# Order of the work around the paired 3x3 convolutions of a pre-activation block, and both rows' products in one tile

## The chip, the cores and the metric

The kernel runs on one core of a Trainium2 chip. The metric is the device time of one execution in microseconds, here the median of three runs. The engines are TensorE (PE in the profile, with its weight loads as PEld), VectorE (DVE), ScalarE (ACT), GpSimd (POOL) and SyncE (SP, which issues DMA transfers).

## The reference

A batch of 8 images with 512 channels of 32 x 32 pixels goes through group norm, a 1x1 convolution (cv1), two bottleneck layers, each with a 3x3 convolution, an attention over the 1024 pixels and a 1x1 convolution (m_cv2), and a closing 1x1 convolution (cv2). All of it is fp32.

```python
def _gn(v, G=32, eps=1e-5): ...        # group norm: (v - mean) / sqrt(var + eps)
def cbs(x, w, p, pad):                 # conv, batch norm with fixed statistics, SiLU
    return silu(bn_eval(conv2d(x, w, pad), p))
def bot_attention(x, qkv_w, rw, rh):   # HEADS = 4, HD = 64, hw = 1024
    q, k, v = conv2d(x, qkv_w, 0) ...
    logits = einsum('bhdi,bhdj->bhij', q, k + (rw + rh)) * HD ** -0.5
    return einsum('bhij,bhdj->bhdi', softmax(logits), v)
t = cbs(_gn(x), cv1_w, cv1_bn, 0)      # 512 -> 512 channels, 1x1
ys = [t[:, :256], t[:, 256:]]
for i in range(2):                     # two layers
    z = cbs(ys[-1], m_cv1_w[i], m_cv1_bn[i], 1)      # 3x3, 256 -> 256
    z = bot_attention(z, m_qkv_w[i], m_rw[i], m_rh[i])
    z = silu(bn_eval(conv2d(z, m_cv2_w[i], 0), m_cv2_bn[i]))
    ys.append(ys[-1] + z)
out = x + cbs(concatenate(ys, axis=1), cv2_w, cv2_bn, 0)   # 1024 -> 512
```

## The kernel before, in words

**Stages.** The images are taken in four pairs (loop `for p in range(NP)`), image a and image b. A pair passes, for layer 0 and then layer 1, these stages: `conv3x3` (line 486) for both images at once; `project_strassen` (684) and `attention_fast` (778) of image a; the same of image b; and `m2` (1021), the 1x1 convolution with its SiLU and the addition to the layer's input, for each image. Between the stages of layer 0 lies cv1 of the next pair's images (`strassen_cv1`, 1140; plain `cv1` in the first pair), and at the end of layer 1 cv2 of both images (`strassen`, 1053, in seven block products), in the last image plain. What the last pair does is the same without a next pair. Layer 1's order is: convolution, project a, attention a, project b, m2 a, attention b, m2 b, with cv2 around it.

**The 3x3 convolution** is of the Winograd kind: input tiles of 6 x 6 pixels are transformed by `tiles_in` (421) on VectorE, the filters by `make_u` (342), and the products of transformed input and filter are summed on TensorE and transformed back on VectorE. `tiles_in` works for one image and one or several of three row indices i; each gives three tiles `v_in` (cp = 0, 1, 2 for the column indices (0, 5), (1, 2), (3, 4)). In `conv3x3` a unit is an output block oc and a row index i, six in a convolution; a unit has two rows. Before, each row takes a tile `ps` of two PSUM banks for its own six products (L520); ACT copies products 2 and 4 (L524), and VectorE takes sum and difference with 1 and 3 (L526, L527) and joins products 0 and 5 (L528). These operate on 128 x 256 elements. Four recombinations (`c_r`, L533 to L536) and the keeping of both rows (`c_k`, L539 and further; output to `z`, L542 to L551) follow. The pool `ps_big` has three tiles of two banks, which all stages share; `ps_av` has one.

**Attention.** `attention_fast` computes 16 pairs of steps per image: logits (L801), exp on ACT (L805), addition of the exponentials on VectorE (L819, L821), products with v (L835). The softmax's denominators are made on TensorE (`sums`, 845), written to DRAM by way of `s_row`, read back as a narrow tile, inverted (`reciprocal` on 128 x 8), written and broadcast back to 128 x 512 (`spread`, 891), and used by `scale` (904, L907). There are four groups; the last one is done without DRAM, by `last_sums` (862), an addition, and a 128 x 512 reciprocal (L943). `behind` is a dictionary of hooks, called at fixed steps of the attention: group g, or (g, quarter).

**What sets the order.** The program text is in the order of the wishes, and a scheduler gives each engine its queue; `tc.issue_after(ins)` puts what is inside behind an instruction. A tile pool with few buffers makes a later tile wait for the release of an earlier one. Filters, weights and new filter blocks share a ring of ten slots (tag `u`); `feed` issues loads of keys on SP, `take` uses them. The first pair also makes the layer-1 filters (`make_u`, with `load_raw`, stored by POOL) and the block sums of the weights. The group norm of the next image (`group_norm`, 614) is stepped by the hooks; its last step, `apply`, normalises on VectorE (L624).

**What the text below touches**: the names above; `first_sum` (678), which forms the first block sum of the projection's input (`t_z`, L681, L732 to L734), and `L697`/`L701`, the products of the projection; `next_cv1` with `begin`, `go_on`, `rest`, the steps of the next image's cv1.

## Time and profile before

| what | value |
|---|---|
| median of three runs | 2467.01 us (2465.4 to 2467.69) |
| the profiled execution's own time | 2468.43 us |
| its span | 2467.0 us |
| mean granted TensorE clock | 0.973 |
| ACT 128 x 1024 exponentials (L805) | 512 of 1023 ns |
| VectorE additions of exponentials (L821) | 384 of 1223 ns |

The span is the time from the first to the last instruction of the profiled execution. A row of the table of costliest groups gives line, engine, operation, output from inputs, sizes and count; after the first bar the busy time in us and the mean duration in ns; after the second the time that the engine sat idle just before these instructions, and what ended most of it. The table by windows gives the busy time of each engine in a stretch, so that a stage can be read by itself. In the text, "layer 0" and "layer 1" are the bottleneck layers, and "a" and "b" the two images of a pair.

### The profile page before, as it was taken

To read this page: it belongs to the slowest core of one execution; us is meant where nothing else is said; L and a number is where in the kernel's file an instruction comes from. 1 tells how busy PE (TensorE), PEld (TensorE's weight loads), DVE (VectorE), ACT (ScalarE), POOL (GpSimd) and SP (SyncE) were. 2 spreads that over 40 slices of the span, in tenths; PEclk is the share of its full clock that TensorE was granted. 3 is DMA by queue.
4 is the path that set the end of the run, shared out by engine and by line. 5 is a ranking of instruction groups with operands and counts; after the bars stand their busy time and mean duration, and the time that the engine had idled before them with its cause. 6 is when DMAs were issued, how large, how long until landed. Compare 5 with 4: busy or idle time off the path is not lost.

```text
span 2467.0 us, 40820 instructions
## 1 busy us (share of the span) xinstructions
PE 2261.3 (92%) x16378; PEld 1107.8 (45%) x16378; DVE 1991.3 (81%) x2942; ACT 1013.0 (41%) x1345; POOL 177.1 (7%) x405
## 2 busy tenths in 40 slices
PE   6697979899998999999999998989999898989998
PEld 2362424634447343644346443463444733363433
DVE  6988786888868989887788889888786879597763
ACT  4134333265313545255511555436531364425541
POOL 4101110000010010000011000000001000000002
PEclk9898989999999999999999999999999999999999
DMA  8533423521245041522145223341124502141103
GB/s 309 184 119 126 158 93 110 183 66 65 67 159 192 28 170 41 178 78 78 32 145 185 82 74 113 117 156 57 40 78 155 182 23 78 49 157 36 53 27 121
DMA packets 126534, 268.93 MB, mean 109 GB/s; under 512 B 33440, under 2 KB 62560, under 8 KB 125312
## 3 DMA queue, kind: packets, MB, share of 16 engines
q1 hardware_dynamic: 102256, 181.41, 22.8%
q0 software_dynamic: 24080, 84.82, 9.4%
q8 instruction: 131, 2.15, 0.3%
q14 instruction: 67, 0.55, 0.1%
HBM read 197.10 MB, written 69.07 MB: 108 GB/s over the span
## 4 chain that ended last, share of the span: by engine, by line
PE 56%; DVE 21%; issue 16%; ACT 3%; DMA 2%; POOL 1%; SPq 0%; DVEq 0%; POOLq 0%; ACTq 0%
PE av_ps L835 14%; PE l_ps L801 13%; PE c L1047 8%; PE c_new L1047 4%; PE p_ps L697 4%; PE m_ps L1027 4%; PE ps L416 3%; PE pv_ps L701 1%; PE c_ps L520 1%; DVE acc L821 1%; PE x_ps L1153 1%; DVE w_d L466 1%; DVE v_in L469 1%; PE s_ps L852 1%; DVE c_t L526 1%
## 5 line engine op out<-in xcount | busy, mean ns | idle before, releaser
L805 ACT ACTIVATE pt<-l_ps 128x1024 f32<-128x1024 f32 x512 | 495.7, 1023 | 352.8 <-PE l_ps L801 317.1
L821 DVE TENSOR_TENSOR acc<-acc,pt 128x1024 f32<-128x1024 f32 x384 | 469.6, 1223 | 79.5 <-ACT pt L805 54.6
L801 PE MATMUL l_ps<-q,kr 64*64 64x512 f32 x4096 | 494.5, 597 | 28.6 <-ACT pt L805 25.8
L835 PE MATMUL av_ps<-pt,vT 64*64 64x512 f32 x4096 | 492.5, 597 | 16.0 <-DVE z L843 11.3
L801 PEld LDWEIGHTS l_ps<-q,kr 64*64 64x64 f32 x4096 | 158.4, 134 | 305.4 <-issue 247.1
L520 PE MATMUL c_ps<-v_in,u 128*64 128x128 f32 x4320 | 254.4, 282 | 38.8 <-DVE c_e L528 38.2
L835 PEld LDWEIGHTS av_ps<-pt,vT 64*64 64x64 f32 x4096 | 158.6, 134 | 291.5 <-issue 234.8
L520 PEld LDWEIGHTS c_ps<-v_in,u 128*64 128x64 f32 x4320 | 249.1, 143 | 47.6 <-ACT c_m L524 41.9
L697 PE MATMUL p_ps<-t_z,sq 128*128 128x512 f32 x256 | 130.1, 628 | 27.5 <-DVE c_e L528 19.6
L524 ACT COPY c_m<-c_ps 128x256 f32<-128x256 f32 x96 | 35.2, 370 | 254.1 <-PE c_ps L520 137.1
L1027 PE MATMUL m_ps<-z,m_sb 128*128 128x512 f32 x256 | 113.6, 595 | 0.2
L819 DVE TENSOR_TENSOR acc<-pt 128x1024 f32<-128x1024 f32 x64 | 78.1, 1221 | 38.2 <-ACT pt L805 38.2
L697 PE MATMUL p_ps<-z,sq 128*128 128x512 f32 x192 | 92.2, 604 | 15.3 <-ACT z L397 14.0
L397 ACT ACTIVATE t<-m_ps,bh,sh 128x512 f32<-128x512 f32 x64 | 46.3, 775 | 108.8 <-PE m_ps L1027 108.5
L1027 PEld LDWEIGHTS m_ps<-z,m_sb 128*128 128x128 f32 x256 | 47.8, 190 | 61.7 <-issue 55.0
L697 PEld LDWEIGHTS p_ps<-t_z,sq 128*128 128x128 f32 x256 | 45.8, 200 | 62.7 <-issue 56.1
L701 PEld LDWEIGHTS pv_ps<-sq,z 128*128 128x128 f32 x384 | 51.3, 197 | 33.8 <-issue 18.4
L701 PE MATMUL pv_ps<-sq,z 128*128 128x128 f32 x384 | 53.4, 284 | 10.4 <-DVE z L843 7.7
L907 DVE TENSOR_TENSOR z<-z,rs 128x512 f32<-128x512 f32 x64 | 43.9, 687 | 22.3 <-DMA rs<-r_dram 22.0
L466 DVE TENSOR_TENSOR w_d<-w_rows 128x1024 f32<-128x1024 f32 x48 | 58.6, 1222 | 3.7 <-POOL w_rows L452 1.3
L416 PE MATMUL ps<-x,w 128*128 128x512 f32 x128 | 56.1, 594 | 0.0
L1153 PE MATMUL x_ps<-t_x,sw 128*128 128x512 f32 x128 | 55.6, 592 | 0.0
(276 smaller groups left out, 3228.3 us busy)
## 6 DMA issues: line engine op xcount, KB each, us to landing
u<-u SPq DMA_DIRECT2D x135, 512.0 KB
sq<-sq SPq DMA_DIRECT2D x48, 384.0 KB
x_res<-in_x_dram POOLq DMA_DIRECT2D x63, 256.0 KB, 4.1
x<-in_x_dram SPq DMA_DIRECT2D x28, 512.0 KB
y_in<-y SPq DMA_DIRECT2D x28, 512.0 KB
u<-u_new POOLq DMA_DIRECT2D x54, 256.0 KB, 2.8
rs<-r_dram SPq DMA_DIRECT2D x96, 128.0 KB
v<-v_new POOLq DMA_DIRECT2D x36, 256.0 KB, 3.3
```

The costliest lines, as they stand in the source:

```text
L416: last_product[0] = nc.tensor.matmul(ps[:, half, :], w_of(k), rhs_of(k, half), start=(k == begin), stop=(k == end))
L466: tt(d, e[:, :, 2 : F + 2], e[:, :, 0:F], ALU.subtract)
L520: nc.tensor.matmul(to[o], us[cp][:, k, row, c, o], rhs, start=(k == 0), stop=(k == NM - 1))
L697: nc.tensor.matmul(ps[:, o, :], w[:, o, :], rhs, start=not onto, stop=True, skip_group_check=onto)
L701: nc.tensor.matmul(v[:, ts(j, P)], rhs[:, ts(j, P)], w[:, 2, :], start=j == 0 and not onto, stop=True, skip_group_check=True,)
L801: nc.tensor.matmul(ps[kh * HD : (kh + 1) * HD, hd, :], kr[r, c, o : o + HD], q[r, c, ts(half, HALF)], start=True, stop=True,)
L805: exp = nc.scalar.activation(pt, ps, AF.Exp, scale=SCALE)
L821: ins = nc.vector.tensor_tensor(accs[g], accs[g], pt[i], ALU.add)
L835: nc.tensor.matmul(avs[g][hd * HD : (hd + 1) * HD, kh, :], vT[r, j, o : o + HD], pt[i][r, hd, :], start=(j == 0), stop=(j == NJ - 1),)
L1027: nc.tensor.matmul(pss[oc][:, half, :], m2_sb[:, n, k, ts(oc, P)], ao[:, k, ts(half, HALF)], start=(k == 0), stop=(k == NM - 1),)
L1047: nc.tensor.matmul(ps[:, o, :], w[:, k, ts(o, P)], rhs[part][:, c], start=(k == 0 and not onto), stop=(k == KB - 1), skip_group_check=onto,)
L1153: nc.tensor.matmul(ps[:, o, :], w[:, c, ts(o, P)], rhs[c], start=(c == 0 and not onto), stop=(c == 1), skip_group_check=onto,)
```

## The change

- **Convolution.** The two rows of a unit are now in one tile each for the products 1 to 4 (`inner_ps`, both banks) and for 0 and 5 (`outer_ps`, one bank). TensorE makes products 1 to 4 of both rows first. The ACT copy and the three VectorE operations become 128 x 512 each, half as many. The order in which filters are fed is cp = 1, 2, 0.
- **Input side.** `tiles_in` goes by row index over both images: at the start of the kernel index by index, and at the end of a pair indices 0 and 1 of both images ahead of cv2's last part (`b3`), index 2 behind it.
- **Normalisation.** In the first pair, `group_norm` normalises by eight ACT activations per image, and no longer by four VectorE operations.
- **Filters.** `make_u` yields two or three times per chunk instead of once. One key of the layer-1 filters is made in the first pair's attention a, three between attention a and in attention b; before, two in each.
- **Ends of attention.** Unless `at_once` is set, the last group too goes through `sums`, `spread` and `scale`, each called by the caller. Only attention b of layer 0 keeps the direct form.
- **m2 of image a.** In layer 1, and in layer 0 of the last pair, `sums` is called within the first product of project b (`early`), and `spread`, `scale`, `m2` and the loading of the Exp table after its first half (`middle`). In layer 0 of the other pairs these steps stand between parts of the next image's cv1. At the end of layer 1 cv2's first part is cut in two around them.
- `rs` has four buffers instead of two, and the sums for cv1's Strassen products (`t_x`) are formed after its first products.

The core of the diff:

```diff
-    SLOTS = ((0, 1), (2, 4), (3, 5))
...
-        return [("u", n, oc, i, cp) for oc in range(NM) for i in range(NI) for cp in range(3)]
+        return [("u", n, oc, i, cp) for oc in range(NM) for i in range(NI) for cp in (1, 2, 0)]
...
+            if i < 2:
+                yield last
             nc.scalar.activation(u0, c0, AF.Identity, scale=0.25)
             nc.scalar.copy(u5, c2)
             tt(u2, c0, c2, ALU.add)
             tt(u1, u2, c1, ALU.add)
-            tt(u2, u2, c1, ALU.subtract)
+            yield tt(u2, u2, c1, ALU.subtract)
...
-                    e = act.tile([P, 2, 2, q], F32, tag="rs", name="c3_e", bufs=2)
-                    for row in range(2):
-                        ps = ps_big.tile([P, 2, HALF], F32, tag="big", name="c3_ps")
-
-                        def slot(a, b):
-                            bank, at = divmod(a, 4)
-                            return ps[:, bank, at * q : (at + b - a) * q]
-
-                        for cp in range(3):
-                            for c in range(2):
-                                to = slot(SLOTS[cp][c], SLOTS[cp][c] + 1)
-                                for k in range(NM):
-                                    rhs = vs[i, cp][:, c].rearrange(
-                                        "p g (r t k s) -> p g r t k s", r=2, t=NT, k=NM
-                                    )[:, :, row, :, k]
-                                    for h in range(2):
-                                        o = slice(h * HD, (h + 1) * HD)
-                                        nc.tensor.matmul(
-                                            to[o], us[cp][:, k, row, c, o], rhs, start=(k == 0), stop=(k == NM - 1)
-                                        )
-                        m24 = act.tile([P, 2, q], F32, tag="h", name="c3_m", bufs=2)
-                        nc.scalar.copy(m24, slot(4, 6).rearrange("p (a q) -> p a q", a=2))
-                        m13 = slot(2, 4).rearrange("p (a q) -> p a q", a=2)
-                        tt(m[:, row, 0::2], m13, m24, ALU.add)
-                        tt(m[:, row, 1::2], m13, m24, ALU.subtract)
-                        stt(
-                            e[:, row].rearrange("p a q -> p (a q)"), slot(0, 2), -6.0,
-                            m[:, row, 0:2].rearrange("p a q -> p (a q)"), ALU.mult, ALU.add,
-                        )
+                    e = act.tile([P, 2, 2, q], F32, tag="rs", name="c3_e", bufs=4)
+                    inner_ps, outer_ps = (
+                        ps_big.tile([P, 2, HALF], F32, tag="big", name="c3_ps") for _ in range(2)
+                    )
+
+                    def slots(ps, bank):
+                        return ps[:, bank, : 4 * q].rearrange("p (r a q) -> p r a q", r=2, a=2)
+
+                    places = {
+                        1: (inner_ps, 0, 0), 2: (inner_ps, 1, 0), 3: (inner_ps, 0, 1), 4: (inner_ps, 1, 1),
+                        0: (outer_ps, 0, 0), 5: (outer_ps, 0, 1),
+                    }
+                    for cps in ((1, 2), (0,)):
+                        for row in range(2):
+                            for cp in cps:
+                                for c in range(2):
+                                    ps, bank, at = places[CPS[cp][c]]
+                                    to = slots(ps, bank)[:, row, at]
+                                    for k in range(NM):
+                                        rhs = vs[i, cp][:, c].rearrange(
+                                            "p g (r t k s) -> p g r t k s", r=2, t=NT, k=NM
+                                        )[:, :, row, :, k]
+                                        for h in range(2):
+                                            o = slice(h * HD, (h + 1) * HD)
+                                            nc.tensor.matmul(
+                                                to[o], us[cp][:, k, row, c, o], rhs,
+                                                start=(k == 0), stop=(k == NM - 1),
+                                            )
+                    m24 = act.tile([P, 2, 2, q], F32, tag="h", name="c3_m", bufs=2)
+                    nc.scalar.copy(m24, slots(inner_ps, 1))
+                    tt(m[:, :, 0::2], slots(inner_ps, 0), m24, ALU.add)
+                    tt(m[:, :, 1::2], slots(inner_ps, 0), m24, ALU.subtract)
+                    stt(
+                        e.rearrange("p r a q -> p r (a q)"),
+                        slots(outer_ps, 0).rearrange("p r a q -> p r (a q)"), -6.0,
+                        m[:, :, 0:2].rearrange("p r a q -> p r (a q)"), ALU.mult, ALU.add,
+                    )
...
-        def group_norm(xts):
+        def group_norm(xts, on_act=False):
...
-            yield apply(range(NX), gm, gn_rstd(dev)[0])
+            gr, _, _ = gn_rstd(dev)
+            if not on_act:
+                yield apply(range(NX), gm, gr)
+                return
+            shift = small.tile([P, NX], F32, tag="dev", name="shift")
+            nc.gpsimd.tensor_tensor(shift, gm, gr, ALU.mult)
+            nc.gpsimd.tensor_scalar(shift, shift, -1.0, None, ALU.mult)
+            for c in range(NX):
+                for half in range(NH):
+                    part = xts[c][:, ts(half, HALF)]
+                    nc.scalar.activation(part, part, AF.Identity, scale=gr[:, c : c + 1], bias=shift[:, c : c + 1])
+            yield
...
-        def project_strassen(n, z, w, t):
+        def project_strassen(n, z, w, t, early=None, middle=None):
...
+            product(ps_a, ps_v[:, 0], w["11"], b11, between=early)
...
+            if middle:
+                middle()
...
+            if not at_once:
+                with tc.issue_after(added.ins):
+                    scale(g - 1, rss.pop(g - 1))
+                return SimpleNamespace(
+                    sums=lambda: s_drams.update({g: sums(g)}),
+                    spread=lambda: rss.update({g: spread(g, s_drams[g])}),
+                    scale=lambda: scale(g, rss.pop(g)),
+                )
...
-        for g in range(G):
-            s.tiles_in(Y1[g], putter(vs, g), [0])
-        for g in range(G):
-            s.tiles_in(Y1[g], putter(vs, g), [1, 2])
+        ecs = [{}, {}]
+        for i in range(NI):
+            for g in range(G):
+                s.tiles_in(Y1[g], putter(vs, g), [i], ecs[g])
...
+        def hooks(norms, every=1):
+            calls = {}
+            for g in range(NG):
+                for at in range(4):
+                    key = (g, at) if at else g
+                    calls[key] = [step_norm] if key in norms else []
+                    if (4 * g + at) % every == 0:
+                        calls[key].append(step_u)
+            return {key: (lambda fs: lambda: [f() for f in fs])(fs) for key, fs in calls.items()}
+
+        NORMS = (1, 2, (2, 2), 3)
+        if p == 0:
+            more_u = filters([(0, 0, 0)])
...
-        scaled, check = s.attention_fast(qkv, z[:, :, 0], at_of(ia, 0), behind)
-        if p == 0:
-            for made in chunks:
-                pass
-        last = s.m2(0, z[:, :, 0], Y1[0], lambda oc, half: inner(Y2[0], oc, half))
-        if more:
-            nxt.rest()
-        with tc.issue_after(last.ins):
-            check()
+            before = behind[3, 2]
+            behind[3, 2] = lambda: (before(), make_sq(1, q_tiles, [t[:, j] for t in q_sums for j in range(2)]))
+        end = s.attention_fast(qkv, z[:, :, 0], at_of(ia, 0), behind)
+        for made in more_u:
+            pass
...
+            more_u = filters([(0, 1, 1), (1, 0, 1), (1, 1, 1)])
+
+        def m2_a():
+            return s.m2(0, z[:, :, 0], Y1[0], lambda oc, half: inner(Y2[0], oc, half))
+
+        if more:
+            end.sums()
+            nxt.go_on()
+            nxt.sums()
+            end.spread()
+            nxt.rest(0)
+            end.scale()
+            last = m2_a()
+            for i in range(1, 4):
+                nxt.rest(i)
...
+            for _ in range(12):
+                step_u()
...
+            def middle():
+                end.spread()
+                end.scale()
+                m2_a()
+                with tc.issue_after(s.silu_in[-1].ins):
+                    s.table_of(AF.Exp)
+
+            feed(units(1)[:6])
+            qkv = s.project_strassen(
+                0, z[:, :, 1], take_blocks("sq", 0, 1, SQ_NAMES), t, early=end.sums, middle=middle
+            )
...
+        def middle():
+            end.spread()
+            end.scale()
+            s.m2(1, z[:, :, 0], Y2[0], lambda oc, half: img(y3a[half][:, oc, :]))
+            if more:
+                nxt.finish()
+                nxt.keep()
+            with tc.issue_after(s.silu_in[-1].ins):
+                s.table_of(AF.Exp)
+
+        qkv = s.project_strassen(
+            1, z[:, :, 1], take_blocks("sq", 1, 1, SQ_NAMES), t, early=end.sums, middle=middle
+        )
...
+        end.sums()
+        a1_more()
+        a2()
+        end.spread()
+        end.scale()
...
-            s.tiles_in(Y1[0], putter(vs, 0))
+            ecs = [{}, {}]
+            for g in range(G):
+                s.tiles_in(Y1[g], putter(vs, g), [0, 1], ecs[g])
             b3(bottom)
             feed(units(0))
-            s.tiles_in(Y1[1], putter(vs, 1))
+            for g in range(G):
+                s.tiles_in(Y1[g], putter(vs, g), [2], ecs[g])
```

## The prediction

> **What bounds the kernel now.** I read the page first, by engine. TensorE is busy for 92% of the span, VectorE for 81%. Both are too high for one bound; which one rules must be read stage by stage.
>
> ```profile
> PE 2261.3 (92%) x16378; PEld 1107.8 (45%) x16378; DVE 1991.3 (81%) x2942; ACT 1013.0 (41%) x1345; POOL 177.1 (7%) x405
> ```
>
> TensorE sits idle for 2467 - 2261 = 206 us, and no edit here removes a matmul, so about 200 us is the ceiling of any gain. Next I read the costliest groups for what ended TensorE's idle time.
>
> ```profile
> L520 PE MATMUL c_ps<-v_in,u 128*64 128x128 f32 x4320 | 254.4, 282 | 38.8 <-DVE c_e L528 38.2
> L697 PE MATMUL p_ps<-t_z,sq 128*128 128x512 f32 x256 | 130.1, 628 | 27.5 <-DVE c_e L528 19.6
> L524 ACT COPY c_m<-c_ps 128x256 f32<-128x256 f32 x96 | 35.2, 370 | 254.1 <-PE c_ps L520 137.1
> L907 DVE TENSOR_TENSOR z<-z,rs 128x512 f32<-128x512 f32 x64 | 43.9, 687 | 22.3 <-DMA rs<-r_dram 22.0
> ```
>
> The convolution (L520) and the projection after it (L697) wait for L528, the last VectorE read of a convolution tile: VectorE is late, and TensorE waits for a free tile. Two small groups of the table of all lines give further prices, and the third says how the first pair's convolution waits for its input side:
>
> ```profile
> L526 DVE TENSOR_TENSOR c_t<-c_ps,c_m 128x256 f32<-128x256 f32 x96 | 40.3, 420 | 8.1 <-ACT c_m L524 7.5
> L943 DVE RECIPROCAL rs<-rs 128x512 f32<-128x512 f32 x16 | 53.6, 3352 | 0.4
> L520 PE MATMUL c_ps<-v_in,u_new 128*64 128x128 f32 x288 | 23.5, 340 | 23.7 <-DVE v_in L469 18.3 <-DVE c_e L528 4.5 <-DVE v_in L482 0.9
> ```
>
> Last, the table of busy time by window. The rows are the first pair's layer-0 convolution, its attentions a and b, and the second pair's layer-0 convolution, project a and attention a.
>
> ```profile
> 84.90:148.60 63.70, 39.47 (x578) 38.10 (x577) 60.52 (x116) 8.34 (x17) 2.18 (x12) 0.79 0.44 155
> 173.40:250.70 77.30, 63.35 (x546) 22.55 (x545) 69.45 (x116) 38.89 (x51) 10.40 (x19) 0.89 0.30 101
> 309.50:392.30 82.80, 64.62 (x546) 22.36 (x545) 71.92 (x117) 37.69 (x50) 10.20 (x18) 0.88 0.24 82
> 743.60:781.80 38.20, 33.53 (x578) 32.92 (x577) 37.53 (x79) 8.59 (x18) 2.17 (x4) 0.96 0.69 234
> 781.80:805.20 23.40, 19.03 (x90) 11.86 (x92) 17.71 (x32) 10.41 (x16) 0.00 (x0) 1.00 0.35 107
> 805.20:862.70 57.50, 57.50 (x545) 21.56 (x545) 52.30 (x69) 35.72 (x41) 1.03 (x1) 1.00 0.08 22
> ```
>
> Columns: window, length, then busy time of PE, PEld, DVE, ACT, POOL, then the granted clock. Convolutions are bound by VectorE (37.5 of 38.2 us); an ordinary attention by TensorE (57.5 of 57.5); the first pair's two attentions by VectorE, which carries 17 to 20 us more there than in an ordinary one. Adding up TensorE's gaps in the trace by stage gives 62.6 us in the eight convolutions, 60.7 in the projections, 48.3 in the attentions (32.1 of them in the first pair's layer-0 two), 22.5 in the opening, and under 0.3 in cv1, m2 and cv2 together.
>
> [...] successive operations overlap: starts lie 0.335 us apart at 128x256 and 0.60 at 128x512. I use those, as merging two operations then saves 0.07 us, not 0.15. [...] in the trace u_new's stores land after 2.8 us, and the two-transfer way from reciprocal through r_dram to rs takes 6.2 to 6.4 us until the scaling starts. [...] the trace's silu of that form takes 0.775. I use 0.775.
>
> **Part 1: the convolutions.** Per unit six VectorE operations of 128x256 become three of 128x512: 6 x 0.335 - 3 x 0.60 = 0.2 us, times 6 units = 1.3 us per convolution; two ACT copies become one, and L526's wait for them (8.1 us over eight convolutions) mostly goes, 0.9 us each. The rest is order. In the second pair VectorE starts its first subtraction 9.3 us after TensorE's first product (752.9 against 743.6), since a whole input tile of image b and the adds of cv2 stand before it. In the new order the input-side work of index 2 is in the queue earlier, and about 4.5 us of cv2 adds remain. From there I count 18 merged operations x 0.6 = 10.8, 24 recombinations x 0.46 = 11.0 and 21 others x 0.6 = 12.6: 34.4 us, and about 0.9 for waits on ACT. Project a's product that needs image a's last silu-and-sum chain starts at 48.3 us now and at 4.5 + 34.4 + 0.9 = 39.8 then: 8.5 us for each of three. The floor is not reached: TensorE's own 32.3 us of products plus the first project products lie below that. Layer-1 convolutions already have a shorter start; the same count gives 39.4 to 35.3, 4.1 us for each of three, and 5.8 for the first pair's, whose gap is longer. The first pair's layer-0 convolution stalls once for 13.1 us on v_in (L469); index by index for both images its tiles arrive in the order in which the units use them, but unit 0 now needs v12 and v34 before v05. I take 6.4 us (bounds -1 to 14). Sum: 25.5 + 12.3 + 5.8 + 6.4 = 50.0 us.
>
> **Part 2: the first pair's attentions.** The normalisation leaves VectorE (4 x 0.81 = 3.2 us per image) for ACT (8 x 0.775 = 6.2), which is busy for half of the stage. Attention a makes one filter key instead of two. A key is three chunks of six operations x 0.335, two of them with three more of 0.56: 9.4 us, 3.1 a chunk. VectorE falls from 69.5 by 12.6 to 57, below TensorE's 61 to 64 at this clock (0.89). So 77.2 becomes about 63: 14 us. Attention b sheds 3.2 us, and of its three keys so much is done ahead of it that about 1.5 chunks fewer remain (4.7); the finer pieces let its waits of 5 to 6 us in one go shrink, by an estimated 3: 82.8 to about 72, 11 us; VectorE remains its bound. Together 25 us.
>
> **Part 3: where the displaced filters go.** About 4.5 chunks, 14 us of VectorE, now stand in its queue between attention a and project b, ahead of the reciprocal and scaling for m2 a. The ring of ten slots holds few free ones there, so a chunk may wait for its store; the next raw load stands on SP's queue in front of s_dram. TensorE has 14 us of cv1 as cover; what exceeds it is lost. Bounds 0 to 10 us; I take 6, because both queues are in the way.
>
> **Part 4: the ends of attention.** At 12 of 16 ends the sums' add (0.69) and the 3.35 us reciprocal are replaced by s_row, s_dram, a 0.2 us reciprocal, r_dram and rs. VectorE loses 46 us of busy time, which mostly lies beside TensorE's work and is worth nothing. The new chain: s_row to the issue of sums_all 1.7, landing about 2, reciprocal and transfers 6.3, scaling 0.7: about 10.8 us. Work that hides it: cv1 or cv2 products in front of m2's second half, 14.3 to 14.8 us. The cover lasts while the chain is under 14.5; past that every end pays the excess. In the second and third pair's layer 0, m2 a moves 3 us later in TensorE's order, and project b there waits for the adds that follow m2: 3 us each, 6 us (0 to 8).
>
> **Part 5: m2 inside the projection** (layer 1, and the last pair's layer 0). m2 and its silu now stand between the two halves of project b, so the attention that follows starts without them: attention b of layer 1 has 1.57 to 1.61 us idle at its start in each pair, the last pair's project b and attention b 8.8 + 2.6. Behind the waiting m2 on VectorE are the projection's adds, on ACT its copies. I take 1 us gained per layer-1 attention (4, bounds -4 to 9) and 6 in the last pair (0 to 9). POOL's and SP's further moves are ahead of need: 0.
>
> **Sum.** 50 + 25 - 6 - 6 + 4 + 6 = 73 us. The profiled execution took 2468.4 us with a span of 2467.0; it becomes 2395.4. It lies 1.4 us above the median of the runs (2467.0), so I predict 2394.
>
> **The rivals.** *VectorE keeps the bound and takes part 1 back.* A merged tile gets free only after a copy and three operations at 512; if what comes early in the convolution is lost waiting in the projection (60.7 us idle today), half of 50 is lost: 2419. For: L697 already waits 19.6 us for L528. Against: the count above has less VectorE work, not only an earlier start. Chance 0.20. *The displaced filters block the first pair:* part 3 at 10 us and attention b unchanged: 2394 + 4 + 11 = 2409. Chance 0.10. *More than I grant:* the first convolution's 13 us stall goes whole, attention b reaches 63, and part 4 costs nothing: 7 + 9 + 6 = 22 more, 2372. For: these gaps are in the trace. Chance 0.15. *Slower: the transfers of the ends.* If s_dram, r_dram and rs queue on SP behind weight loads waiting for ring slots, the chain passes its cover at 12 ends. To eat 73 us it must overrun by 6.1 at each, a chain of 20.6 us, twice what the trace shows; at 22 us it costs 12 x 7.5 = 90: 2484. For: the waits of SP show u loads held 26 us for L520. Against: today's spreads cross the same queue in 6.3 us. Chance 0.04. *The order is other than written*, the scheduler keeping the old place of the input side: only merging, part 2 and the rest, about 2430. Chance 0.01, as the instruction order of the changed kernel shows the move. My own case has 0.50.
>
> **Numbers.** The case at 2394 spans 2380 to 2408 by its bounds. The range leaves out the slower case and the ends of the larger gain: 2368 to 2432. A change of 0.2% (5 us) is about what a measurement of this kernel can tell from none; faster by more 0.95, within 0.01, slower 0.04.
>
> **What would show it.** Convolution windows of the second pair near 34 us with VectorE's first subtraction about 4.5 us after the first product; L697's wait for L528 much smaller; attention a of the first pair near 63, b near 72; the reciprocal at 128x512 four times, not 16; no wait of m2 for rs in TensorE's rows. A wait of m2 on rs or s_dram at all ends, or projection windows longer than today's, would make the prediction wrong.

## The result and the profile after

The changed kernel took 2451.43 us (median of four runs, 2449.15 to 2452.53) against 2467.35 us for the kernel before beside it: a ratio of 0.9936 with a 95% interval of 0.9919 to 0.9953. That is 16 us less. The forecast was 73 us less, with a range that ended at 2432. The profiled execution took 2449.15 us, with a span of 2447.6. The page after, by engine:

```profile
PE 2254.5 (92%) x16378; PEld 1101.8 (45%) x16378; DVE 1933.5 (79%) x2766; ACT 1012.0 (41%) x1301; POOL 178.4 (7%) x409
```

VectorE lost 58 us of work, TensorE's idle time only 13 us (205.7 to 193.1). The other 7 us of the shorter span are TensorE's busy time, for the same 16378 matmuls. From the costliest groups after (L528, L717, L533, L825, L829, L931 and L1058 are L520, L697, L524, L801, L805, L907 and L1027 of before), and last the logits' row of before:

```profile
L829 ACT ACTIVATE pt<-l_ps 128x1024 f32<-128x1024 f32 x512 | 496.4, 1025 | 370.2 <-PE l_ps L825 332.9
L825 PE MATMUL l_ps<-q,kr 64*64 64x512 f32 x4096 | 493.3, 597 | 49.4 <-ACT pt L829 46.7
L528 PE MATMUL c_ps<-v_in,u 128*64 128x128 f32 x4320 | 245.9, 277 | 16.3 <-ACT c_m L533 16.3
L717 PE MATMUL p_ps<-t_z,sq 128*128 128x512 f32 x256 | 128.5, 619 | 19.4 <-DVE c_t L535 19.4
L1058 PE MATMUL m_ps<-z,m_sb 128*128 128x512 f32 x256 | 114.6, 600 | 8.9 <-DVE z L931 8.9
L533 ACT COPY c_m<-c_ps 128x512 f32<-128x512 f32 x48 | 28.0, 584 | 211.6 <-PE c_ps L528 83.8
L801 PE MATMUL l_ps<-q,kr 64*64 64x512 f32 x4096 | 494.5, 597 | 28.6 <-ACT pt L805 25.8 <-ACT t L397 2.1 <-DVE kr L719 0.7
```

The convolution's idle time fell from 38.8 to 16.3 us, that of the projection's products with `t_z` from 27.5 to 19.4 (its products with `z` went from 15.3 to 17.2). But the logits (L825) now wait 46.7 us for exponentials, where they waited 25.8 us before, and m2 waits 8.9 us for the last scaling, where it waited 0.2. By window, in the order of before's rows (the first pair's convolution, attentions a and b; the second pair's convolution, project a, attention a), and last the last pair's layer-0 attention b:

```profile
83.00:143.30 60.30, 39.81 (x577) 38.62 (x577) 59.15 (x100) 7.80 (x12) 2.19 (x12) 0.77 0.50 168
166.70:241.20 74.50, 62.36 (x545) 21.27 (x546) 60.67 (x91) 43.39 (x55) 5.57 (x11) 0.93 0.11 35
314.50:402.00 87.50, 65.22 (x545) 21.79 (x546) 67.58 (x107) 43.49 (x57) 9.59 (x18) 0.90 0.23 77
749.80:781.30 31.50, 31.50 (x577) 31.33 (x577) 29.51 (x51) 7.88 (x12) 1.08 (x2) 1.00 0.81 274
781.30:804.40 23.10, 19.05 (x90) 11.72 (x88) 17.42 (x29) 10.03 (x15) 0.00 (x0) 1.00 0.33 99
804.40:862.00 57.60, 57.60 (x546) 21.66 (x546) 52.40 (x69) 35.80 (x41) 1.04 (x1) 1.00 0.08 22
2034.50:2114.20 79.70, 59.79 (x538) 19.71 (x538) 67.14 (x84) 36.56 (x41) 5.34 (x13) 0.87 0.16 57
```

The second pair's convolution now has TensorE busy in all of its 31.5 us. The first pair's attentions have much less VectorE work than before (60.7 for 69.5, 67.6 for 71.9 us), and yet a is hardly shorter and b is longer. The rows also show that the busy time of an attention's matmuls (x545 or x546) is not fixed: 57.6 us where the granted clock is 1.00, 62.4 at 0.93, 65.2 at 0.90. In these three the lower clock goes with a TensorE that waits more (0, 12.1 and 22.3 us); but project a's row has 4.1 us of waiting in 23.1 at a clock of 1.00, and the last row 59.8 us of busy time at 0.87. What causes what was not tried.

Below, "the stretch" is the time from attention a to attention b of a pair's layer 0 (cv1, m2 of a, project b). Stage lengths, from TensorE's instructions in both traces, against the forecast:

| stage | before | after | change | forecast |
|---|---|---|---|---|
| first pair, convolution 0 and project a | 88.5 | 83.7 | -4.8 | -6.4 |
| first pair, attention a | 77.3 | 74.5 | -2.8 | -14 |
| first pair, the stretch (cv1, m2 a, project b) | 58.8 | 73.3 | +14.5 | +6 |
| first pair, attention b | 82.8 | 87.5 | +4.7 | -11 |
| pairs 2 to 4, convolution 0 and project a, sum | 185.3 | 164.8 | -20.5 | -25.5 |
| all pairs, convolution 1 and project a, sum | 254.4 | 244.9 | -9.5 | -18.1 |
| pairs 2 and 3, the stretch, sum | 110.1 | 114.7 | +4.6 | +6 |
| last pair, project b with m2 a | 39.8 | 26.7 | -13.1 | |
| last pair, attention b | 60.3 | 79.7 | +19.4 | -6, both together |
| all pairs, layer 1, project b, m2 a, attention b, sum | 354.0 | 347.2 | -6.8 | -4 |

The rest (opening, cv2, the other ends) gave 5 us. So four places hold the shortfall: the first pair's attentions (27 us short), its stretch (8.5), the last pair's attention b (12) and the convolutions (15).

What stands behind three of them can be read from ScalarE. Its groups in the first pair's attention a, after:

```profile
L829 ACT ACTIVATE pt<-l_ps 128x1024 f32<-128x1024 f32 x32 | 30.9, 1024 | 21.3 <-PE l_ps L825 21.3
L654 ACT ACTIVATE x<-x,shift,gr 128x512 f32<-128x512 f32 x8 | 5.8, 802 | 6.1 <-POOL shift L650 6.1
...
L364 ACT ACTIVATE u_new<-ypad 128x256 f32<-128x256 f32 x3 | 1.2, 412 | 7.5 <-DVE ypad L354 5.3 <-DVE ypad L350 2.3
```

The first of the eight normalisations stands 6.1 us waiting for GpSimd's `shift`, the filter copies 7.5 us for VectorE, and the exponentials behind them in ScalarE's queue wait too; the normalisation then takes 5.8 us of its own. ScalarE's and TensorE's rows at that place:

```profile
227.89 5.76 ACT L654 ACTIVATE x<-x,shift,gr 128x512 f32<-128x512 f32 x8 [6.13 <-POOL shift L650]
233.56 2.81 ACT L829 ACTIVATE pt<-l_ps 128x1024 f32<-128x1024 f32 x3
234.61 1.98 PE L825 MATMUL l_ps<-q,kr 64*64 64x512 f32 x8 [7.17 <-ACT pt L829]
```

The waits of the copies are older than the change. Their rows in attentions a and b before, and in b after:

```profile
L363 ACT ACTIVATE u_new<-ypad 128x256 f32<-128x256 f32 x5 | 2.1, 417 | 21.9 <-DVE ypad L355 9.4 <-DVE ypad L351 8.9 <-DVE u_new L368 2.3
L363 ACT ACTIVATE u_new<-ypad 128x256 f32<-128x256 f32 x5 | 2.1, 417 | 28.0 <-DMA u<-u_new 11.0 <-DVE ypad L351 8.9 <-DVE ypad L355 8.1
L364 ACT ACTIVATE u_new<-ypad 128x256 f32<-128x256 f32 x4 | 1.7, 415 | 19.1 <-DVE ypad L354 12.2 <-DVE ypad L350 6.9
```

In the timeline of attention b in the last pair after, TensorE's and ScalarE's rows:

```profile
2036.84 1.09 PE L825 MATMUL l_ps<-q,kr 64*64 64x512 f32 x8 [0.46 <-DVE q L785]
2057.38 1.99 PE L825 MATMUL l_ps<-q,kr 64*64 64x512 f32 x8 [19.45 <-ACT pt L829]
```

```profile
2055.01 1.28 ACT L829 ACT_TABLE_LOAD   x1 [25.97 <-DVE w_g L450]
2056.30 3.02 ACT L829 ACTIVATE pt<-l_ps 128x1024 f32<-128x1024 f32 x3
```

The first exponential waits for VectorE's input tiles of layer 1: all three parts of `tiles_in` for image a now stand between project b and attention b.

### The profile page after: what moved, and what is told of

It reads as the page before. It is cut to its first block, busy times and chain, and to the rows that moved or that the text cites. A ratio compares the mean times of both kernels' runs of the same rounds, so it can differ in the third digit from the quotient of the medians.

```text
span 2447.6 us, 40591 instructions
## 1 busy us (share of the span) xinstructions
PE 2254.5 (92%) x16378; PEld 1101.8 (45%) x16378; DVE 1933.5 (79%) x2766; ACT 1012.0 (41%) x1301; POOL 178.4 (7%) x409
## 4 chain that ended last, share of the span: by engine, by line
PE 63%; DVE 25%; issue 5%; DMA 3%; ACT 3%; POOL 1%; SPq 0%; DVEq 0%; POOLq 0%; ACTq 0%
PE av_ps L859 14%; PE l_ps L825 14%; PE c L1078 8%; PE c_new L1078 6%; PE p_ps L717 5%; PE m_ps L1058 4%; DVE acc L845 3%; PE c_ps L528 3%; PE ps L417 3%; PE x_ps L1189 2%; PE pv_ps L723 2%; PE s_ps L876 1%; DVE c_e L536 1%; DVE w_d L467 1%; PE p_ps L723 1%
## 5 line engine op out<-in xcount | busy, mean ns | idle before, releaser
L829 ACT ACTIVATE pt<-l_ps 128x1024 f32<-128x1024 f32 x512 | 496.4, 1025 | 370.2 <-PE l_ps L825 332.9
L825 PE MATMUL l_ps<-q,kr 64*64 64x512 f32 x4096 | 493.3, 597 | 49.4 <-ACT pt L829 46.7
L825 PEld LDWEIGHTS l_ps<-q,kr 64*64 64x64 f32 x4096 | 158.2, 134 | 323.3 <-issue 250.0
L528 PE MATMUL c_ps<-v_in,u 128*64 128x128 f32 x4320 | 245.9, 277 | 16.3 <-ACT c_m L533 16.3
L528 PEld LDWEIGHTS c_ps<-v_in,u 128*64 128x64 f32 x4320 | 242.9, 140 | 22.8 <-ACT c_m L533 17.4
L717 PE MATMUL p_ps<-t_z,sq 128*128 128x512 f32 x256 | 128.5, 619 | 19.4 <-DVE c_t L535 19.4
L1058 PE MATMUL m_ps<-z,m_sb 128*128 128x512 f32 x256 | 114.6, 600 | 8.9 <-DVE z L931 8.9
L533 ACT COPY c_m<-c_ps 128x512 f32<-128x512 f32 x48 | 28.0, 584 | 211.6 <-PE c_ps L528 83.8
L717 PE MATMUL p_ps<-z,sq 128*128 128x512 f32 x192 | 93.5, 618 | 17.2 <-ACT z L398 10.9
L931 DVE TENSOR_TENSOR z<-z,rs 128x512 f32<-128x512 f32 x64 | 44.1, 689 | 70.8 <-DMA rs<-r_dram 70.7
L1058 PEld LDWEIGHTS m_ps<-z,m_sb 128*128 128x128 f32 x256 | 48.7, 192 | 68.7 <-issue 56.8
L717 PEld LDWEIGHTS p_ps<-t_z,sq 128*128 128x128 f32 x256 | 45.4, 197 | 54.7 <-issue 52.3
L467 DVE TENSOR_TENSOR w_d<-w_rows 128x1024 f32<-128x1024 f32 x48 | 58.8, 1225 | 3.6 <-DVE w_rows L462 0.5
L717 PEld LDWEIGHTS p_ps<-z,sq 128*128 128x128 f32 x192 | 34.2, 193 | 58.0 <-issue 35.2
```

Of the source, the lines that this page charges most:

```text
L467: tt(d, e[:, :, 2 : F + 2], e[:, :, 0:F], ALU.subtract)
L528: nc.tensor.matmul(to[o], us[cp][:, k, row, c, o], rhs, start=(k == 0), stop=(k == NM - 1),)
L717: nc.tensor.matmul(ps[:, o, :], w[:, o, :], rhs, start=not onto, stop=True, skip_group_check=onto)
L825: nc.tensor.matmul(ps[kh * HD : (kh + 1) * HD, hd, :], kr[r, c, o : o + HD], q[r, c, ts(half, HALF)], start=True, stop=True,)
L829: exp = nc.scalar.activation(pt, ps, AF.Exp, scale=SCALE)
L1058: nc.tensor.matmul(pss[oc][:, half, :], m2_sb[:, n, k, ts(oc, P)], ao[:, k, ts(half, HALF)], start=(k == 0), stop=(k == NM - 1),)
```

## The experiments

Runs of one group share a chip and its runs of the kernel before, so comparisons across groups go by the ratio to before (one per mille is 2.5 us). Stage lengths are those of the one profiled execution. How well they repeat can be seen in the four runs below whose edits leave the first pair's attentions alone: attention a took 73.9 to 75.0 us there, the stretch 73.1 to 74.6, attention b 87.4 to 87.9.

**The last pair's input tiles.** First, other memory for `v_new`, with the order untouched (`-` is the changed kernel, `+` the run, also below; `...` stands for lines left out):

```diff
-            v_new[i, cp] = t = act.tile([P, 2, 2 * P], F32, tag="pt", name="v_new", bufs=6)
+            tag, bufs = ("pt", 6) if more else ("x", NX)
+            v_new[i, cp] = t = act.tile([P, 2, 2 * P], F32, tag=tag, name="v_new", bufs=bufs)
```

> The changed kernel, but the last pair's nine transformed input tiles v_new lie in tiles of tag x and no longer in tag pt, which the exponentials of attention b need; the instruction order stays. Theory A (the 19.45 us gap at the start of the last pair's attention b is a wait of ScalarE for pt tiles that v_new holds): the gap goes; VectorE still has 18 us of tile work ahead of its additions, so attention b comes down from 79.6 us only to 65 to 75, and the whole by 5 to 15 us, near 2440. Rival B (the gap is VectorE's load itself): attention b stays at 78 to 80 us, the whole within 3 us of the changed kernel.

Measured: 2450.84 us, ratio 0.9941 (0.9924 to 0.9957), no change; attention b took 79.1 us. The exponentials did start at once, but only three pairs of steps: ScalarE's row in the timeline of this run reads

```profile
2065.60 2.86 ACT L829 ACTIVATE pt<-l_ps 128x1024 f32<-128x1024 f32 x3 [17.09 <-DVE acc L843]
```

The wait for a tile was real, and with it gone the same 18 us of VectorE work hold the first addition, and so the release of the exponentials' tiles. So theory A, a gap made by the wait for memory, fell, and rival B held: it is VectorE's queue. Second, the same memory and the three parts called from steps of the attention:

```diff
-            for i in range(NI):
-                s.tiles_in(Y2[0], put_away, [i], ec)
-                store(i)
...
+            behind |= {(0, 2): tiles_of(0), (1, 2): tiles_of(1), (2, 2): tiles_of(2)}
```

> As the run before, and the three parts of the tile work are called from steps of attention b instead of ahead of it. Theory A: no block is left, VectorE's 67 us of work set the stage: attention b near 66 to 69 us, the whole 11 to 14 us under the changed kernel, near 2438. Rival B (the load of VectorE wherever it stands): attention b within 3 us of 79.6 us. A third, that the work is taken up by the slack of TensorE's 57.5 us, would give 58 to 60 us and 20 us less.

Measured: 2435.76 us, 0.9877 (0.9860 to 0.9893), 14.6 us under the changed kernel by the ratios; attention b 66.3 us, VectorE busy for 62.1 of it. Theory A holds: the order cost 13 us of that stage. That VectorE's load makes the other 9 above the 57.5 us of an ordinary attention is argued from its 62.1 us, not tried.

**The normalisation.** Back on VectorE in the first pair:

```diff
-            norm = s.group_norm(xs, direct)
+            norm = s.group_norm(xs)
```

> The changed kernel with the first pair's normalisation on VectorE as before. Theory A (the eight ScalarE activations wait 5 to 6 us for shift with the exponentials queued behind them, and cost 5.8 us of ScalarE): attentions a and b of the first pair fall from 74.5 and 87.5 us by 4 to 8 us each, the whole by 6 to 14 us. Rival B (VectorE is the bound of these stages, as the prediction had it): each grows by about 3 us, the whole by 4 to 7 us.

Measured: 2438.53 us, 0.9888 (0.9872 to 0.9905), 11.8 us under the changed kernel. Attention a fell to 65.1 us and b to 82.9, as theory A has it. So the move that took 3 us from VectorE cost these stages 9.4 and 4.6 us. The stretch grew by 4.1 us in this run, to 77.3, which takes back part of that.

**The filters.** Placed and stepped as before, two keys in each attention and nothing between:

```diff
-            more_u = filters([(0, 0, 0)])
-        behind = hooks(NORMS, 2) | {NG: begin_cv1(0, Y1[0], ia + 2)}
+            more_u = filters([(0, 0, 0), (0, 1, 1)])
+        behind = hooks(NORMS, 99) | {NG: begin_cv1(0, Y1[0], ia + 2)}
...
-            for _ in range(12):
-                step_u()
...
```

> The changed kernel with the first pair's filter blocks made as before: two keys in attention a, two in attention b, one yield a chunk, none between. Theory A (the displaced filters block ScalarE, SP and the ring between attention a and m2 a): the stretch from the end of attention a to project b falls from 47.7 to 36 to 39 us, attention b from 87.5 to 80 to 84, attention a grows from 74.5 to 78 to 84; the whole 4 to 14 us lower. Rival B (the stretch is long because the last sums go by DRAM, not because of the filters): 45 us or more there, and the whole 0 to 8 us higher.

Measured: 2452.02 us, 0.9945 (0.9929 to 0.9962), no change as a whole. The stretch up to project b fell from 47.7 to 35.3 us, with no wait of m2, and the whole stretch from 73.3 to 58.8, as long as before the change: the chain by DRAM is hidden there when no filters stand in it. Attention a grew to 84.4 us, and b stayed, at 88.8. Theory A is right about the stretch and wrong about the whole: moved, the filters cost the same time elsewhere. Next, the two copies of a layer-1 filter chunk on GpSimd:

```diff
-            nc.scalar.activation(u0, c0, AF.Identity, scale=0.25)
-            nc.scalar.copy(u5, c2)
...
+                nc.gpsimd.tensor_scalar(u0, c0, 0.25, None, ALU.mult)
+                nc.gpsimd.tensor_copy(u5, c2)
```

> The changed kernel, but the two outer copies of each layer-1 filter chunk (u0 and u5, on ScalarE before) are done by GpSimd. Theory A (the copies wait for VectorE's mid rows at the head of ScalarE's queue, with the exponentials behind them; the profile shows 7.5 us in attention a of the first pair and 19.1 in b): attention a falls from 74.5 by 3 to 7 us, b from 87.5 by 8 to 15, the stretch between them by 2 to 6; the whole by 12 to 25 us. Rival B (VectorE's load is what binds and the waits of ScalarE only mirror it): within 4 us of the changed kernel. A third, that GpSimd is slower per copy than the 0.4 us of ScalarE and the stores leave later, would show as waits for u_new and a loss of up to 5 us.

Measured: 2444.53 us, 0.9914 (0.9892 to 0.9935), 5.4 us under the changed kernel, the intervals just overlapping. Attention b fell by 7.2 us (theory A asked for 8 to 15), attention a by 1.8, the stretch not at all. The direction in attention b is A's, the size is not, and by the whole alone rival B (within 4 us) is not excluded. With the normalisation still on ScalarE, attention a keeps a wait of 6.0 us for `shift`, and b one of 5.1.

**The convolution.** Each part alone: rows in tiles of their own again (the block shown in the change, reversed); the input side's order undone at both places; and the merged tile in the kernel before.

```diff
-        for i in range(NI):
-            for g in range(G):
-                s.tiles_in(Y1[g], putter(vs, g), [i], ecs[g])
+        for g in range(G):
+            s.tiles_in(Y1[g], putter(vs, g), [0])
+        for g in range(G):
+            s.tiles_in(Y1[g], putter(vs, g), [1, 2])
```

> The changed kernel with the convolution's rows in tiles of their own again, in the old product order; all the rest as changed. Theory A (the prediction's count: fewer operations and fewer waits for ScalarE's copy give about 2.2 us per convolution): 14 to 20 us more than the changed kernel, over all eight. Rival B (with the earlier input side TensorE's 31.6 us are the floor and VectorE has slack again): 0 to 8 us more, only in the layer-1 convolutions.

> The changed kernel with the input tiles made in the order of before, at the start and at the end of each pair; the merged tile stays. Theory A (the prediction's: VectorE begins 4.8 us late in three convolutions, and the first pair's loses its order): 12 to 22 us more than the changed kernel, all in the layer-0 convolutions. Rival B (the merged tile lets TensorE run far enough ahead to absorb it): 0 to 6 us more.

> The kernel before with the merged tile alone. Theory A (operations and waits count): 14 to 20 us under the kernel before. Rival B (the order of the input side is the gain, the tile alone can't use it): 0 to 8 us under it.

Measured: rows apart 2467.48 us, 1.0005 (0.9995 to 1.0015), 17 us above the changed kernel; input side as before 2465.82 us, 0.9998 (0.9987 to 1.0009), 15 us above; merged tile alone 2450.48 us, 0.9935 (0.9916 to 0.9954), 16 us under the kernel before. Theory A holds in all three, in size too. The second pair's layer-0 convolution shows how they join: 38.2 us before, 36.3 with the merged tile alone, 32.7 with the order alone, 31.5 with both, where TensorE has no gap left. With project a, which follows it, pairs 2 to 4 come to 185.3, 180.0, 170.8 and 164.9 us, so here the two gains add. The order does nothing in layer 1 (38.3 for 38.0); there the merged tile is the whole gain.

**Together.** The hooks, the normalisation on VectorE and the GpSimd copies in one kernel; then the first pair's attention a ending directly, without transfers; then the second and third pairs' too:

```diff
-        end = s.attention_fast(qkv, z[:, :, 0], at_of(ia, 0), behind)
+        soon = direct and more
+        if soon:
+            behind[NG + 1] = lambda: (nxt.go_on(), nxt.sums())
+        end = s.attention_fast(qkv, z[:, :, 0], at_of(ia, 0), behind, at_once=soon)
...
```

What is left out calls m2 a at once where `soon` holds. In the third of these, `soon` is `more`.

> The changed kernel with three edits together: the last pair's tile work in steps of attention b (as tiles_in_hooks), the normalisation on VectorE (as norm_vector) and the two filter copies on GpSimd (as copies_gpsimd). Theory A (three separate blocks of an engine's queue, so the gains of 15.7, 12.9 and 6.9 us add): 2414 to 2418 us. Rival B (normalisation and copies are one wait of ScalarE seen twice, so freeing one leaves the other bound by VectorE): 2421 to 2427 us.

> The run before, and the first pair's attention a of layer 0 ends without transfers, as the kernel before does. Theory A (there the way by DRAM takes 26 us, not 10.8, since s_dram, r_dram and rs move behind filter and weight loads): the stretch from attention a to attention b falls from 73 to 60 to 64 us, the whole 9 to 13 us under the run before. Rival B (filter operations ahead on VectorE hold m2 anyway): under 4 us.

> The run before, and the second and third pairs' attention a of layer 0 end without transfers too. Theory A (the later place of m2 a costs project b 3 us in each, as the prediction had it): 4 to 7 us under the run before. Rival B (the later place costs nothing, since project b is bound by the adds and tile work of VectorE anyway; the reciprocals of 3.35 us come on top): 0 to 4 us above it.

Measured: 2421.32, 2407.00 and 2400.49 us; ratios 0.9818 (0.9803 to 0.9833), 0.9766 (0.9751 to 0.9781) and 0.9741 (0.9728 to 0.9755). By its time the first lies in rival B's range, at the edge; by ratios, the three gains add to 0.9807, just inside the interval. The whole can't tell the two theories apart. The stages can: attentions a and b lost 26.6 us together, where the normalisation alone gave 14.0 and the copies alone 9.0, so these are two waits and not one seen twice. The attentions are at the 63 and 72 us of the prediction (first and third row; the stretch is the second):

```profile
170.00:232.70 62.70, 57.93 (x544) 21.21 (x544) 58.78 (x87) 35.74 (x41) 12.83 (x15) 1.00 0.12 42
232.70:313.00 80.30, 58.27 (x176) 28.16 (x172) 53.12 (x96) 18.11 (x27) 23.22 (x42) 0.87 0.57 199
313.00:385.70 72.70, 61.32 (x545) 22.52 (x544) 69.27 (x111) 35.71 (x41) 18.64 (x24) 0.95 0.25 85
```

but the stretch grew to 80.3 us, 7 us more than in the changed kernel, and took back that much of the gain. The direct end takes 14.3 us off the whole (A: 9 to 13), while the stretch itself only fell to 71.8 us, not to 60 to 64, and attention b fell by 2.1; the rest of the difference lies in stages that the edit doesn't touch. Within m2 TensorE still idles 7.5 us, now for VectorE's addition of the sums, which stands behind filter chunks, as do the reciprocal and scaling after it. So A is right about the transfers, B about what comes next. The later ends gave 6.5 us, A's size, but not all of it where A puts it: the stretches of the second and third pairs fell by 2.4 and 2.0 us, and the first pair's, which this edit leaves alone, by 3.1.

Last, in that kernel the filter steps behind m2 a:

```diff
-            for _ in range(12):
-                step_u()
+            with tc.issue_after(last.ins):
+                for _ in range(12):
+                    step_u()
```

> The run direct_ends, with the filter steps between the first pair's attentions issued behind m2 a. Theory A (the filter chunks ahead of the sums' addition, the reciprocal and the scaling on VectorE hold m2 a, 7.5 us of TensorE's idle time): the stretch from attention a to attention b falls from 68.7 to 58 to 62 us; attention b or project b takes back what VectorE then has to do later, 0 to 8 us; the whole 2 to 10 us under direct_ends. Rival B (VectorE's sum over the stretch and attention b is what counts, wherever the chunks stand): within 2 us of direct_ends.

Measured: 2400.65 us, 0.9730 (0.9716 to 0.9744), overlapping the run without. The stretch and attention b, first without, then with the edit:

```profile
231.60:300.30 68.70, 57.90 (x178) 27.70 (x180) 61.03 (x103) 19.28 (x28) 23.06 (x44) 0.95 0.66 236
300.30:370.90 70.60, 61.35 (x545) 21.83 (x545) 66.00 (x102) 35.07 (x40) 17.55 (x22) 0.95 0.24 80
```

```profile
232.10:289.80 57.70, 55.06 (x172) 26.70 (x172) 46.88 (x80) 19.14 (x28) 20.27 (x33) 1.00 0.47 169
289.80:373.20 83.40, 65.99 (x545) 21.86 (x545) 79.72 (x130) 35.51 (x40) 25.87 (x34) 0.90 0.42 145
```

The stretch loses 11 us and attention b gains 12.8. VectorE is busy for 127.0 of 139.3 us in one, 126.6 of 141.1 in the other. This is B's case: the two stages together don't get shorter, and a wait of m2 ahead of the same VectorE work is no cost of its own. That VectorE's sum binds them is argued from this; 12 to 14 us in which it is idle are left open. The best version is thus the one with direct ends, 2.6% under the kernel before; the last edit can't be told from it.

## Why the prediction was wrong

**Part 1, right in kind, 15 us too large.** VectorE's first operation on the products (a sum, which the prediction calls a subtraction) comes 4.4 us after the first product in the second pair (754.1 against 749.7), as said. VectorE then works without a wait to 790.1, and its chain still sets the end. TensorE has no gap in the convolution, but waits before and at the product of project a that ends the count:

```profile
786.45 1.96 PE L717 MATMUL p_ps<-t_z,sq 128*128 128x512 f32 x4 [2.30 <-DVE c_t L535]
791.04 3.70 PE L717 MATMUL p_ps<-z,sq 128*128 128x512 f32 x8 [1.75 <-ACT z L398]
```

So "The floor is not reached" holds, and the mis-sized term is the count of 34.4 us: the same operations took 36.0. Most of that is one spacing. The operation behind a unit's last recombination starts 0.47 us after it where it reads something else, and 0.67 us where it reads the result. The count took 0.46 for all. Before, 24 of the 48 units were of the longer kind; with the rows merged 43 are, and all six of this convolution: 0.2 us six times. The product starts at 41.3 us, not 39.8, and the three pairs gained 6.9, 6.2 and 7.3 us, not 8.5. In layer 1 the same count gave 35.3 us from VectorE's first operation to the product; it took 37.2, for 39.4 before. That leaves 2.2 us, what the prediction itself had put merging at, and the stages gained 1.7 to 2.0 us for 4.1.

**Part 2, the step that failed.** "So 77.2 becomes about 63" followed VectorE's load alone. The load did fall, to 60.7 us (57 in the sum), and the stage only to 74.5. The price of the normalisations was nearly right (0.80 us each; 0.775 in the sum, the mean of the silu of m2, L397 at 128x512, in the trace before). What failed is the wait: the step took an engine that is "busy for half of the stage" as free room. The eight normalisations brought their 6.1 us of waiting for `shift` into ScalarE's queue ahead of the exponentials; undoing this gave 9.4 us of attention a and 4.6 of b. The filter copies had waited there before (21.9 and 28.0 us in the trace before), and the prediction left them where they were, with no term for it in a and 3 us in b: waits of 7.5 us in a and 19.1 in b remained. With the normalisations back on VectorE and the copies gone as well, the stages came to 62.7 and 72.7 us. In b this is most of it: without the copies' move it stands at 82.9, as long as before. That attention a then meets the forecast 63 is in part luck: the prediction had TensorE at 61 to 64 us there, and it took 57.9, at a granted clock of 1.00 and not 0.89.

**Part 3, right, and too small.** The stretch grew by 14.5 us for 6 taken, 8.9 of it m2's wait for rs. The run with the filters elsewhere removed all 14.5. VectorE's rows around that wait, in the timeline after:

```profile
261.23 0.20 DVE L919 RECIPROCAL rc<-sums_all 128x8 f32<-128x8 f32 x1
274.66 0.69 DVE L931 TENSOR_TENSOR z<-z,rs 128x512 f32<-128x512 f32 x1 [13.23 <-DMA rs<-r_dram]
```

The way from the reciprocal to the scaling took 13.4 us there, for 6.3 in the calculation; SP issued weight loads of 512 KB between r_dram and rs, and the filters' stores were under way. At the same end in the run with the filters elsewhere, with no such load between, it took 5.2 us; rs was issued 1.4 us after r_dram there (263.86 to 265.26), and 5.2 us after it in the changed kernel (262.14 to 267.31). The trace before already had one like it, in the first pair's layer 1: 13.0 us from 521.7 to 534.7, with loads of `y_in` issued on SP in between. The other ten at which the scaling waited took 5.1 to 7.2 us, and the prediction's 6.2 to 6.4 left the long one out. Earlier in the chain ScalarE's queue cost time too: the copy to `s_row` came at 254.7, 6 us after the sums, behind filter copies that waited 4.9 us for VectorE.

**Part 4, right at all ends but one.** The rival in which transfers pass their cover came true in this one place, at 26.5 us from the sums (248.15) to the scaling. At the other eleven ends m2 waits for nothing. The count has about 2 us for the landing of sums_all; where the reciprocal waited for it, it came 2.5 and 4.7 us after the issue in the trace before (372.55 to 375.05, 517.04 to 521.70), and in the trace after 1.5 to 1.6 us at five ends, 3.1 and 4.1 at two. The price of 3 us for the later m2 in the second and third pairs was right (2.6 and 2.0; taken back by the last of the direct ends).

**Part 5, right in layer 1 (6.8 us for 4), wrong in the last pair.** There it looked at project b and m2 alone, which did gain 13.1 us. The part moved with them, all of `tiles_in` behind project b, was not costed: its 18 us stand ahead of the attention's first addition, and the attention lost 19.4. With the tile work in hooks attention b is only 6.0 us longer than before (66.3 for 60.3), so that run gains 13.1 - 6.0 = 7.1 us in the two, near the forecast.

## What to carry to other kernels

Before work is moved to an engine that has time, list what each moved instruction waits for and what stands behind it in that engine's queue, and list the waits that stand there already: here each of them held the exponentials, on an engine that was busy for half of the stage. When something is taken out of one stage, follow where its VectorE work goes: over two neighbouring stages with VectorE busy nine tenths of the time, moving 14 us of it from one to the other saved nothing. And when operations are merged or reordered, count them with the spacing that the new neighbours will have: an operation that had filled a gap may be gone (0.67 us here in place of 0.47).

## What the hardware showed beyond that

GpSimd took 0.89 to 1.60 us for the scaled 128 x 256 copy (four of them, from 244 to 261 us of the run with the GpSimd copies) that ScalarE did in 0.41 us. In the run with the first direct end, which has these copies too, three of VectorE's filter operations averaged 0.447, 0.458 and 0.495 us between 229.5 and 275.4 us; in the changed kernel all six averaged 0.417 to 0.422 us over the whole run. The cause was not tried. VectorE's next operation started 0.47 us after a unit's last 128 x 256 recombination where it read something else (29 times in the two traces), 0.67 us where it read the result (67 times). A transfer of 4 KB and a broadcast took 5.2 us together at an end with no load between them, and 13.4 us at the same end beside loads of 512 KB and filter stores.
